# The last three groups of a graph network kernel: sums streamed 32 columns wide, and their place among the last updates

## The chip, the cores and the metric

The kernel runs on one core of one Trainium2 chip. The core has TensorE (PE in the profile, its weight loads shown apart as PEld), VectorE (DVE), ScalarE (ACT), GpSimd (POOL) and SyncE (SP, which here only issues transfers). Every engine works through its own list of instructions in order and waits on semaphores for the others. The metric is the device time of one execution in microseconds (us), as the median of several runs; less is better.

## The reference

One layer of message passing over 12,500 nodes with 64 features and 200,000 edges, which are sorted by destination, then a residual and a layer norm:

```python
msg_in     = concat([x[src], x[dst], edge_attr_32])            # 64 + 64 + 32 features
messages   = relu(msg_in @ mW1 + mb1) @ mW2 + mb2              # 160 -> 128 -> 64
aggregated = segment_sum(messages, dst, 12500)                 # 12500 x 64
update     = relu(concat([x, aggregated]) @ uW1 + ub1) @ uW2 + ub2
out        = layernorm(x + update)                             # over 64 features
```

All of it is float32. Because the sum over edges and the second matrix of the message network commute, the kernel sums the 128 hidden values of the edges per node and applies `mW2` afterwards, once per node.

## The kernel before, in words

**Groups.** The edges are cut into 1563 tiles of 128, and six tiles make a group: groups 0 to 260, the last with three tiles. Since destinations are sorted, the destinations of one tile lie within a window of 32 consecutive nodes. The rows of the sources are gathered from a table in DRAM on GpSimd's queue.

**A group's life.** `edge_part(s)` (L413, L416) makes the parts of the hidden values that come from the destination and the edge features, as products into PSUM (`pc`). `node_part(s)` adds the gathered source part; for the groups from 255 on VectorE does the addition itself (`added_here`, L452) and clips at zero (L455; for the short group 260 ScalarE clips, L457). `collect(s)` then sums the group's edges into their nodes: for each tile a product of a row of ones with the 0/1 selection matrix gives the counts (L502, tile `cnt`), and a product of the hidden values `h` (128 edges x 128 values, the loaded weights) with the selection (the streamed columns) gives the sums (L506, tile `sums`). In float32 each product appears as two records in the profile, so a full group's sums are x12. Where in `sums` the window lies is read from a list at run time.

**The streamed columns.** The 32 columns of a tile's selection lie in `band`. `widened` builds an access pattern that reads them and, `WIDE` - 1 = 2 further times, 32 columns of zeros from elsewhere in `band`, so that 96 columns are streamed and the 64 columns behind the window get zeros added.

**Updates.** The nodes are finished in 36 updates (K = 36; update u in the code). Update K-3 covers the nodes of groups 251 to 254, K-2 those of 255 to 257, K-1 (the last, 256 nodes wide) those of 258 to 260. An update goes through a chain of functions: `close_counts` and `close_sums` copy counts and sums from PSUM (L527, L533, VectorE); `carry(u+1)` hands what overlaps to the next update's sums (L521, L522, TensorE); `from_nodes` and `update` make the first layer from the nodes and counts (L565) and from the sums (L558); `activated` is the ReLU (L570, ScalarE, into `hTu`); `residual` makes the second layer and the residual (L578 from the nodes, L580 from `hTu`), centred, into the PSUM tile `cps`, which all updates share; `squares` (L587, ScalarE), `statistics` (L596, VectorE), `deviation` (L602, ScalarE) and `norm` (L608 and L610, VectorE) are the layer norm; `store` (L617) issues the store on SP's queue.

**What sets the order.** Nothing schedules these instructions: the order in which the functions are called is the order of each engine's list. Up to group 257 a loop makes it; for the last three groups (258 is `FINAL`) and the last three updates it is written out call by call. So a place in this list is a place in the queue of each engine that the called function uses.

Of the kernel before, what the change touches and what calls it, by code (L numbers as in the profile page):

```python
# [10 lines left out]
F32 = mybir.dt.float32  # L11
# [19 lines left out]
WIN = 32  # L31
# [17 lines left out]
WIDE = 3  # L49
# [9 lines left out]
def opener(t):  # L59

    return t - t % SUP % shared(t // SUP)
# [15 lines left out]
SBASE = (33556480, 33554432)  # L77
CBASE = 33566720
PACE = ((3, 0.474), (50, 0.501), (130, 0.479), (170, 0.465), (261, 0))
FINAL = 258  # L80
# [49 lines left out]
def gnn_kernel(ctx: ExitStack, tc: tile.TileContext, x1T, x, eT, e_rows, src, src_row, dst, dst_row, wlist, wrow, wnext, whalf,  # L130
# [24 lines left out]
    nc = tc.nc  # L155
# [8 lines left out]
    K = len(UPD)  # L164
# [53 lines left out]
    def tiles(s):  # L218
        return range(s * SUB, min((s + 1) * SUB, NT))
# [28 lines left out]
    with tc.tile_pool(name="work", bufs=2) as work, tc.manual_schedule():  # L248
# [172 lines left out]
        def node_part(s):  # L421

            n = len(tiles(s))
            added = None
            pc = pcs.pop(s)
            h = work.tile([P, 2, SUB // 2, DH], F32, name="h")
            if s < XG:
                xt = xs.pop(s)
                for i in range(n):
                    k, b = divmod(i, 2)  # L430
                    q = 64 * b
                    nc.tensor.matmul(pc[:, b, k, :], xt[q:q + 64, k, :], w1a[q:q + 64], start=False,
                                     stop=i + 2 >= n)
                nc.scalar.activation(h, pc, AF.Relu)
            else:
                a = xg.pop(s)[0].rearrange("p (b k) f -> p b k f", b=2)
                if s >= SUMMED:
                    added_here(s, n, h, a, pc)
                elif n == SUB:
                    m = SUB // 2 - (s in COPIED)  # L440
                    for b in range(2):
                        added = nc.tensor.matmul(pc[:, b, :m], ident, a[:, b, :m], start=False, stop=True)  # L442
                    late.append((h, pc))
            hs[s] = h
            return added

        def added_here(s, n, h, a, pc):

            m = SUB // 2 - (s in COPIED)
            blocks = [(slice(0, 2), m)] if n == SUB else parts(n)  # L450
            for b, m in blocks:
                nc.vector.tensor_tensor(h[:, b, :m], a[:, b, :m], pc[:, b, :m], op=ALU.add)  # L452
            for b, m in blocks:
                if n == SUB:
                    nc.vector.tensor_scalar(h[:, b, :m], h[:, b, :m], 0.0, None, op0=ALU.max)  # L455
                else:
                    nc.scalar.activation(h[:, b, :m], h[:, b, :m], AF.Relu)  # L457
            if n == SUB and m < SUB // 2:
                nc.vector.tensor_scalar(h[:, :, m:], pc[:, :, m:], 0.0, None, op0=ALU.max)
# [24 lines left out]
        def collect(s):  # L484

            n = len(tiles(s))
            g, j = divmod(s, SUP // SUB)
            k0 = j * SUB
            u = period[s]
            ends = s == NSUB - 1 or period[s + 1] != u  # L490
            if s == 0 or period[s - 1] != u:
                opened(u)
            ps, pn = sums[u]
            h = hs.pop(s)
            at = [t for t in listed(s) if t < NT]
            cs, ws = ([found[at.index(opener(t))] for t in tiles(s)]
                      for found in (places(wcnt, s, at, CBASE), places(woff, s, at, SBASE[u % 2])))
            pn8, ps8 = pn.bitcast(U8), ps.bitcast(U8)
            if s == 0 or period[s - 1] != u:
                nc.tensor.matmul(pn, zero_b[:, 0:1], zero_b, start=True, stop=False)  # L500
            for i in range(n):
                nc.tensor.matmul(pn8[:, bass.ds(cs[i] - CBASE, 4 * WIN)].bitcast(F32), one, SB[g][:, k0 + i, :, 1], start=False,  # L502
                                 stop=ends and i == n - 1)
            made = []
            for i in range(n):
                made.append(nc.tensor.matmul(ps8[:, bass.ds(ws[i] - SBASE[u % 2], 4 * WIDE * WIN)].bitcast(F32), h[:, i % 2, i // 2, :], widened(g, k0 + i),  # L506
                                        start=False, stop=ends and i == n - 1))
            return made

        def widened(g, t):  # L510

            a = g % 3 * SEL + t * WIN
            v = band[:, a:a + WIN]
            return bass.AP(v.tensor, v.offset, [v.ap[0], [(ZTOP - a) // 2, WIDE], [1, WIN]])

        def carry(u):
# [12 lines left out]
        def close_sums(u):  # L529

            ps, _ = sums.pop(u)
            n = UV if u + 1 < K else width(u)
            nc.vector.tensor_copy(sums_s[u % 2][:, :n], ps[:, :n])  # L533
            shut[u] = ps
# [25 lines left out]
        def from_nodes(u, pu=None):  # L560

            n = width(u)
            if pu is None:
                pu = psum.tile([DH, UW], F32, name="sums")[:, :n]
            nc.tensor.matmul(pu, uz, xw[u % 2][:, :n], start=True, stop=False)  # L565
            pus[u] = pu

        def activated(u):

            nc.scalar.activation(hT[:, :width(u)], pus.pop(u), AF.Relu, bias=ub1_s)  # L570
# [3 lines left out]
        def residual(u):  # L574

            py = cps[:, YC:].rearrange("p (i d) -> p i d", d=D)
            for i in range(blocks(u)):
                nc.tensor.matmul(py[:, i], xw[u % 2][:, i * P:(i + 1) * P], ux, start=i == 0, stop=False)  # L578
            for i in range(blocks(u)):
                nc.tensor.matmul(py[:, i], hT[:, i * P:(i + 1) * P], u2c, start=False, stop=i + 1 == blocks(u))  # L580
            ys[u] = py
# [23 lines left out]
        def norm(u):  # L605
            n, y, sd = blocks(u), ys.pop(u), sds.pop(u)
            rs = work.tile([P, UB], F32, name="rs")
            nc.vector.reciprocal(rs[:, :n], sd[:, :n])  # L608
            o = work.tile([P, UB, D], F32, name="y")
            nc.vector.tensor_tensor(o[:, :n], y[:, :n], rs[:, :n].unsqueeze(2).broadcast_to([P, n, D]), op=ALU.mult)  # L610
            us[u] = (us[u], o)
# [3 lines left out]
        def store(u):  # L615
            n0, o = us.pop(u)
            nc.sync.dma_start(out[bass.ds(n0, blocks(u) * P), :].rearrange("(c p) d -> p c d", p=P), o[:, :blocks(u)])  # L617
# [157 lines left out]
        for k, c in enumerate(range(0, NB, NCH)):  # L775
# [20 lines left out]
            if k in (5, 7):  # L796
                g = (k - 5) // 2
# [98 lines left out]
        for s in range(FINAL):  # L896
            g, j = divmod(s, SUP // SUB)
# [85 lines left out]
        deviation(K - 3)  # L983
        update(K - 2)
        activated(K - 2)
        node_part(FINAL + 1)
        norm(K - 3)
        store(K - 3)
        collect(FINAL)
        carry(K - 1)  # L990
        edge_part(FINAL + 2)
        node_part(FINAL + 2)
        residual(K - 2)
        squares(K - 2)
        statistics(K - 2)
        deviation(K - 2)
        collect(FINAL + 1)
        norm(K - 2)
        store(K - 2)
        collect(FINAL + 2)  # L1000
        close_counts(K - 1)
        close_sums(K - 1)
        from_nodes(K - 1)
        update(K - 1)
        activated(K - 1)
# [10 lines left out]
    with tc.If(flag > 0), tc.tile_pool(name="gen", bufs=1) as up:  # L1016
# [28 lines left out]
        with tc.For_i(0, NT, 1) as t:  # L1045
# [31 lines left out]
            h = up.tile([P, DH], F32, name="hg")  # L1077
# [104 lines left out]
```

## Time and profile before

| | |
|---|---|
| median of 3 runs | 2132.84 us (2132.43 to 2137.72) |
| the profiled execution | 2134.32 us in all, 2132.5 us from first to last instruction |
| TensorE busy | 1665.4 us, 78% of the span |
| ScalarE busy | 1583.4 us, 74% |
| GpSimd busy, VectorE busy | 1250.4 us, 59%, and 1162.9 us, 55% |
| mean granted TensorE clock | 0.786 |
| last 15 of these us | the stretch that the change touches |

The rows of the view in time read: start in us from the span's beginning, length in us, engine, line, operation, what is written from what, shapes, number of records; in brackets how long the engine was idle before and what ended that. In the chain of waits each row is one piece of the chain that ended last. A PEld row is a run of weight loads; the distance from its start to the start of the next row divided by its records is what one record of that group takes up on TensorE.

### The profile page before, as it was taken

The numbers are of one execution on the slowest core, as the hardware profiler recorded it, in microseconds if no ns is written. First come the engines' busy times: TensorE is split into PE (matmuls) and PEld (weight loads), VectorE is DVE, ScalarE is ACT, GpSimd is POOL, SyncE is SP. The second block draws the span as 40 slices with busy tenths as digits, with TensorE's granted clock in tenths as the row PEclk, the third lists the DMA queues.
The fourth block names the chain that finished last, engine by engine and source line by source line (L and its number), as shares of the span: only waits on it lengthen the run. The fifth ranks groups of instructions, "written<-read, shape, count | busy, mean of one in ns | idle before, by whom it ended". The sixth has DMA issues, their size and how long they took to land.

```text
span 2132.5 us, 48222 instructions
## 1 busy us (share of the span) xinstructions
PE 1665.4 (78%) x10730; PEld 1259.0 (59%) x10730; DVE 1162.9 (55%) x8400; ACT 1583.4 (74%) x8069; POOL 1250.4 (59%) x1330
## 2 busy tenths in 40 slices
PE   3676887787787787878777878878776888888888
PEld 2564665565565556656656656656555666656666
DVE  2436555555555565565555545555554556555555
ACT  4396977759769688788786877777876868787774
POOL 6665665666665665655655555565556566666660
PEclk8677787787786777777877778787887878788779
DMA  8623333322223232232222323333332333333332
GB/s 227 185 73 85 87 95 90 106 75 80 74 75 81 73 83 75 74 86 78 77 82 81 85 77 89 83 91 84 81 90 75 87 85 94 87 93 88 90 88 54
DMA packets 207647, 190.04 MB, mean 89 GB/s; under 512 B 57813, under 2 KB 173997, under 8 KB 207357
## 3 DMA queue, kind: packets, MB, share of 16 engines
q0 software_dynamic: 42272, 85.08, 15.6%
q1 hardware_dynamic: 150396, 92.86, 15.5%
q10 hardware_dynamic: 14690, 8.99, 1.5%
q8 instruction: 90, 1.47, 0.3%
q14 instruction: 199, 1.63, 0.3%
HBM read 168.76 MB, written 18.02 MB: 88 GB/s over the span
## 4 chain that ended last, share of the span: by engine, by line
PE 50%; issue 16%; DVE 12%; another core or an unknown queue 3%; DVEq 2%; POOL 0%; ACT 0%; DMA 0%; ACTq 0%; POOLq 0%
PE sums L506 16%; PE pc L442 12%; PE pc L413 10%; DVE xc L391 6%; DVE h L466 3%; PE cnt L502 2%; PE cps L580 2%; PE cps L578 2%; DVE l L275 2%; PE sums L565 2%; DVEq L359 2%; PE sums L558 1%; PE pc L416 1%; PE cnt L500 1%
## 5 line engine op out<-in xcount | busy, mean ns | idle before, releaser
L241 POOL DMA_INDIRECT xg<-tab_a,src_s x1273 | 1201.4, 944 | 809.4 <-issue 266.0
L383 ACT ACTIVATE xc<-xtop,xbot 128x1 f32 x7912 | 1501.3, 280 | 172.7 <-issue 149.4
L391 DVE TENSOR_TENSOR xc<-xtop,xbot 128x1 int32 x7576 | 634.7, 154 | 504.9 <-issue 489.6
L506 PE MATMUL sums<-band,h 128*128 128x96 f32 x3126 | 529.7, 322 | 143.1 <-issue 91.3
L506 PEld LDWEIGHTS sums<-band,h 128*128 128x128 f32 x3126 | 466.4, 228 | 172.9 <-issue 106.3
L442 PE MATMUL pc<-xg,band 128*128 128x256 f32 (+1 forms) x988 | 445.8, 581 | 29.1 <-issue 27.5
L413 PE MATMUL pc<-rhs,l 64*128 64x128 f32 x3126 | 366.8, 351 | 79.3 <-issue 66.1
L413 PEld LDWEIGHTS pc<-rhs,l 64*128 64x128 f32 x3126 | 290.0, 235 | 127.0 <-issue 94.9
L466 DVE TENSOR_SCALAR h<-pc 128x768 f32<-128x768 f32 x247 | 235.0, 952 | 167.8 <-remote 62.4
L442 PEld LDWEIGHTS pc<-xg,band 128*128 128x128 f32 x988 | 215.5, 241 | 145.1 <-issue 100.2
L502 PEld LDWEIGHTS <-one 128*1 128x1 bf16 x1563 | 59.0, 81 | 247.2 <-issue 242.7
L275 DVE TENSOR_TENSOR l<-l,cps 128x768 f32<-128x768 int32 (+1 forms) x134 | 127.0, 947 | 136.2 <-remote 31.8
L502 PE MATMUL cnt<-band,one 128*1 128x32 bf16 x1563 | 95.4, 180 | 69.9 <-issue 68.8
L587 ACT ACTIVATE y<-cps 128x256 f32<-128x256 f32 (+1 forms) x36 | 13.6, 379 | 162.2 <-issue 106.8
L570 ACT ACTIVATE hTu<-sums,ub_s 128x416 f32<-128x416 f32 (+1 forms) x36 | 21.6, 600 | 136.0 <-remote 41.7
L416 PE MATMUL pc<-band,xc 64*128 64x128 f32 x484 | 78.3, 314 | 14.5 <-issue 13.3
L283 DVE TENSOR_TENSOR band<-cps,drc 128x384 f32<-128x384 f32 x131 | 71.4, 545 | 20.1 <-PE pc L413 15.8
L675 PE MATMUL pb<-band,xtop 64*128 64x128 f32 x200 | 44.1, 383 | 48.4 <-issue 20.9
L416 PEld LDWEIGHTS pc<-band,xc 64*128 64x128 f32 x484 | 65.2, 228 | 15.6 <-issue 15.5
L675 PEld LDWEIGHTS pb<-band,xtop 64*128 64x128 f32 x200 | 37.4, 276 | 52.5 <-issue 28.7
L241 POOL DMA_INDIRECT xg<-in_x,src_s x48 | 48.0, 1000 | 25.6 <-issue 14.4
L580 PE MATMUL cps<-u2c,hTu 128*128 128x64 f32 x284 | 51.3, 329 | 10.1 <-issue 9.8
(108 smaller groups left out, 636.4 us busy)
## 6 DMA issues: line engine op xcount, KB each, us to landing
l<-in_dst_row SPq DMA_DIRECT2D x262, 96.0 KB
l<-in_eT SPq DMA_DIRECT2D x262, 96.0 KB
xg<-tab_a,src_s POOLq DMA_INDIRECT x1273
rhs<-tab_b SPq DMA_DIRECT2D x361, 32.0 KB
tab_b<-tb SPq DMA_DIRECT2D x13, 512.0 KB
rhs<-tab_b SPq DMA_DIRECT2D x387, 16.0 KB
tab_a<-tb ACTq DMA_DIRECT2D x12, 512.0 KB
out<-y SPq DMA_DIRECT2D x35, 128.0 KB
```

What stands on the lines that cost most here:

```text
L241: ins = nc.gpsimd.indirect_dma_start(out=a[:, i, :] if s < XG else a[:, i // 2, i % 2, :], out_offset=None, in_=A[:, :] if s >= XG else x[ ...
L275: nc.vector.tensor_tensor(l[r], l[r].bitcast(I32), node[r].unsqueeze(2).broadcast_to([r.stop - r.start, SUP // 2, P]), op=ALU.is_equal)
L383: nc.scalar.activation(o[:, e:e + 1], top.bitcast(F32), AF.Identity, bias=bot.bitcast(F32))
L391: nc.vector.tensor_tensor(o[:, e:e + 1].bitcast(I32), top.bitcast(I32), bot.bitcast(I32), op=ALU.bitwise_or)
L413: done = nc.tensor.matmul(pc[:, b, k, :], L[g][q:q + 64, m, :], rhs[g % 2][q:q + 64, w, :], start=k == 0, stop=ends and not copied)
L416: done = nc.tensor.matmul(pc[:, b, k, :], xc[s][q:q + 64], w1a[q:q + 64], start=False, stop=ends)
L442: added = nc.tensor.matmul(pc[:, b, :m], ident, a[:, b, :m], start=False, stop=True)
L466: nc.vector.tensor_scalar(h, pc, 0.0, None, op0=ALU.max)
L502: nc.tensor.matmul(pn8[:, bass.ds(cs[i] - CBASE, 4 * WIN)].bitcast(F32), one, SB[g][:, k0 + i, :, 1], start=False, stop=ends and i == n - 1)
L506: made.append(nc.tensor.matmul(ps8[:, bass.ds(ws[i] - SBASE[u % 2], 4 * WIDE * WIN)].bitcast(F32), h[:, i % 2, i // 2, :], widened(g, k0 + i),
L580: nc.tensor.matmul(py[:, i], hT[:, i * P:(i + 1) * P], u2c, start=False, stop=i + 1 == blocks(u))
L675: nc.tensor.matmul(pb[:, h, i, :], (xbot if h else xtop)[64 * h:64 * h + 64, (c + HB * h + i) * P:(c + HB * h + i + 1) * P], w[64 * h:64 * ...
```

## The change

Three edits, all in the stretch after the loop. `widened` takes the width as an argument, and in the groups from `FINAL` on (258, 259 and 260) it returns the 32 columns of the selection alone. `norm(K-3)` is called before `node_part(FINAL+1)` instead of after it. `collect(FINAL+1)` is called before `residual(K-2)` instead of after `deviation(K-2)`, and `norm(K-2)` and `store(K-2)` are called after `close_sums(K-1)` instead of before `collect(FINAL+2)`. The change computes the same values: what falls away are additions of zeros.

```diff
@@ collect
             for i in range(n):
-                made.append(nc.tensor.matmul(ps8[:, bass.ds(ws[i] - SBASE[u % 2], 4 * WIDE * WIN)].bitcast(F32), h[:, i % 2, i // 2, :], widened(g, k0 + i),
+                wide = 1 if s >= FINAL else WIDE
+                made.append(nc.tensor.matmul(ps8[:, bass.ds(ws[i] - SBASE[u % 2], 4 * wide * WIN)].bitcast(F32), h[:, i % 2, i // 2, :], widened(g, k0 + i, wide),
                                         start=False, stop=ends and i == n - 1))
             return made
 
-        def widened(g, t):
+        def widened(g, t, wide):
 
             a = g % 3 * SEL + t * WIN
             v = band[:, a:a + WIN]
+            if wide == 1:
+                return v
             return bass.AP(v.tensor, v.offset, [v.ap[0], [(ZTOP - a) // 2, WIDE], [1, WIN]])
@@ the calls after the loop
         update(K - 2)
         activated(K - 2)
+        norm(K - 3)
         node_part(FINAL + 1)
-        norm(K - 3)
         store(K - 3)
         collect(FINAL)
         carry(K - 1)
         edge_part(FINAL + 2)
         node_part(FINAL + 2)
+        collect(FINAL + 1)
         residual(K - 2)
         squares(K - 2)
         statistics(K - 2)
         deviation(K - 2)
-        collect(FINAL + 1)
-        norm(K - 2)
-        store(K - 2)
         collect(FINAL + 2)
         close_counts(K - 1)
         close_sums(K - 1)
+        norm(K - 2)
+        store(K - 2)
         from_nodes(K - 1)
         update(K - 1)
         activated(K - 1)
```

Lines below the first edit move by one to three in the changed kernel: L506 becomes L507, and L527, L533, L558, L565, L570, L578, L580, L587, L596, L602, L608, L610 and L617 become L530, L536, L561, L568, L573, L581, L583, L590, L599, L605, L611, L613 and L620.

On TensorE, behind the carry into update K-1 and the edge part of group 260 (L413), the list before has the residual of K-2 (L578, L580; `xw_75` is K-2's node tile):

```order
L521 MATMUL sums<-sums_s_73,band 128x32
L522 ISA
L522 MATMUL cnt<-xw_75,band 1x32
L413 MATMUL pc<-rhs_78,l_81 128x128 x3
L578 MATMUL cps<-ux,xw_75 128x64 x4
L580 MATMUL cps<-u2c,hTu 128x64 x4
L502 LDWEIGHTS one
```

And now, with the counts (L502) and sums (L507) of group 259 done, the residual (L581, L583) comes between them and the counts of group 260:

```order
L502 MATMUL cnt<-band,one 1x32
L507 MATMUL sums<-band,h 128x32 x6
L581 MATMUL cps<-ux,xw_75 128x64 x4
L583 MATMUL cps<-u2c,hTu 128x64 x4
L502 LDWEIGHTS one
```

The residual of K-2 has moved behind group 259's six tiles, and those write 32 columns where they wrote 96.

On VectorE, from the add and clip of group 259 (L452, L455) to the two copies of the last update (L527, L533) the list before is:

```order
L452 TENSOR_TENSOR h<-xg,pc 128x768
L455 TENSOR_SCALAR h<-h 128x768
L608 RECIPROCAL rs<-sd 128x4
L610 TENSOR_TENSOR y<-cps,rs 128x256
L452 TENSOR_TENSOR h<-xg,pc 128x256
L452 TENSOR_TENSOR h<-xg,pc 128x128
L596 TENSOR_REDUCE ss<-y 128x4
L608 RECIPROCAL rs<-sd 128x4
L610 TENSOR_TENSOR y<-cps,rs 128x256
L527 COPY xw_76<-cnt 1x256
L533 COPY sums_s_74<-sums 128x256
```

And now:

```order
L611 RECIPROCAL rs<-sd 128x4
L613 TENSOR_TENSOR y<-cps,rs 128x256
L452 TENSOR_TENSOR h<-xg,pc 128x768
L455 TENSOR_SCALAR h<-h 128x768
L452 TENSOR_TENSOR h<-xg,pc 128x256
L452 TENSOR_TENSOR h<-xg,pc 128x128
L599 TENSOR_REDUCE ss<-y 128x4
L530 COPY xw_76<-cnt 1x256
L536 COPY sums_s_74<-sums 128x256
L611 RECIPROCAL rs<-sd 128x4
L613 TENSOR_TENSOR y<-cps,rs 128x256
```

K-3's norm (the first reciprocal and product) now stands ahead of group 259's add, and K-2's norm behind the last update's copies; K-2's reduction (L596, now L599) is still ahead of the copies. The lists of ScalarE and SP have the same rows in the same order.

## The prediction

> **What bounds the kernel now.** I read the page first, then the chain of waits, then the order in time of one engine after another over the last 20 us, since the change touches nothing before them.
>
> ```profile
> span 2132.5 us, 48222 instructions
> PE 1665.4 (78%) x10730; PEld 1259.0 (59%) x10730; DVE 1162.9 (55%) x8400; ACT 1583.4 (74%) x8069; POOL 1250.4 (59%) x1330
> ```
>
> Over the whole span TensorE is the busiest engine, but what the change is worth must be read from its own stage. The chain of waits over the last 15 us, as start, length and work:
>
> ```profile
> 2119.66 1.03 PE cps L578 x8
> 2120.70 0.89 PE cps L580 x8
> 2121.59 0.23 PE cnt L502 x6
> 2121.83 1.51 PE sums L506 x12
> 2123.33 0.16 PE cnt L502 x3
> 2123.49 0.85 PE sums L506 x6
> 2124.34 0.02 issue
> 2124.37 0.43 DVE sums_s L533
> ...
> 2124.85 0.71 PE sums L558 x2
> ...
> 2125.64 0.48 ACT hTu L570
> ...
> 2128.13 0.29 DVE y L610
> ```
>
> Up to 2124.34 TensorE works without a gap: residual of update K-2 (L578, L580), then the sums of groups 259 (x12: six tiles, two records each) and 260 (x6: three tiles). From there on it is a relay of single steps with one engine working at a time: VectorE's copy of the sums, the last update's products, ScalarE, products, squares, deviation, norm and store. So two things can set the end: how early TensorE gets through its list, and how early VectorE is free for the two copies L527 and L533. Whatever delays the copies or L558 is paid in full.
>
> **The change part by part: narrower streams.** 15 products (30 records) stream 32 columns instead of 96. What one record costs is its distance to the next weight load (PEld rows; at the full clock):
>
> ```profile
> 2110.39 0.30 PEld L502 LDWEIGHTS <-one 128*1 128x1 bf16 x6
> 2110.73 1.41 PEld L506 LDWEIGHTS sums<-band,h 128*128 128x128 f32 x12
> 2112.07 0.97 PEld L578 LDWEIGHTS cps<-ux,xw 128*128 128x128 f32 x8
> ...
> 2118.95 0.52 PEld L413 LDWEIGHTS pc<-rhs,l 64*128 64x128 f32 x6
> 2119.59 0.97 PEld L578 LDWEIGHTS cps<-ux,xw 128*128 128x128 f32 x8
> 2120.48 0.97 PEld L580 LDWEIGHTS cps<-u2c,hTu 128*128 128x128 f32 x8
> 2121.52 0.19 PEld L502 LDWEIGHTS <-one 128*1 128x1 bf16 x6
> 2121.75 1.41 PEld L506 LDWEIGHTS sums<-band,h 128*128 128x128 f32 x12
> 2123.26 0.11 PEld L502 LDWEIGHTS <-one 128*1 128x1 bf16 x3
> 2123.42 0.74 PEld L506 LDWEIGHTS sums<-band,h 128*128 128x128 f32 x6
> ```
>
> Twelve records of L506 with 96 columns take (2112.07 - 2110.73) / 12 = 0.112 us each; eight of L578 with 64 columns take (2120.48 - 2119.59) / 8 = 0.111. A third fewer columns buy nothing: the weight load of 128x128, the same in both, sets the pace. 32 columns therefore save nothing between records, only part of the tail of a group's last one, where somebody waits for its end. The bounds: at least nothing; at most as if cost went with columns, 30 x 0.112 x 2/3 = 2.2 us. I take the end at nothing, because the row with 64 columns lies between 96 and 32 and shows no slope, plus at most 0.08 us of tail for group 260 (64 of 96 columns of a 0.11 us record).
> [...]
>
> **The order on TensorE.** Group 259's products now stand before the residual of K-2, not behind it. Group 259 starts where the residual stood, 2119.59. Its counts (L502) precede the sums by 2110.73 - 2110.39 = 0.34, so its sums start at 2119.93. Followed by L578 a group takes 1.34 (2110.73 to 2112.07): residual at 2121.27, that is 1.68 later than before. The residual and its switch to L502 take 2121.52 - 2119.59 = 1.93: counts of 260 at 2123.20. 0.16 to the sums (2123.26 to 2123.42): 2123.36, 0.06 sooner than now. With the shorter tail, the last product ends 0.06 to 0.14 sooner. That is all TensorE gains: the same records stand there.
>
> **The order on VectorE and ScalarE.** The relay around update K-2 in time, then the last update's first steps:
>
> ```profile
> 2115.03 0.30 ACT L602 ACTIVATE sd<-ss,eps 128x4 f32<-128x4 f32 x1 [0.49 <-DVE ss L596]
> 2121.69 0.38 ACT L587 ACTIVATE y<-cps 128x256 f32<-128x256 f32 x1 [0.92 <-PE cps L580]
> 2122.11 0.42 DVE L596 TENSOR_REDUCE ss<-y 128x4 f32<-128x256 f32 x1 [1.79 <-ACT y L587]
> 2122.89 0.18 DVE L608 RECIPROCAL rs<-sd 128x4 f32<-128x4 f32 x1 [0.36 <-ACT sd L602]
> 2123.16 0.42 DVE L610 TENSOR_TENSOR y<-cps,rs 128x256 f32<-128x256 f32 x1
> 2123.53 0.41 DVE L527 COPY xw<-cnt 1x256 f32<-1x256 f32 x1
> 2124.37 0.42 DVE L533 COPY sums_s<-sums 128x256 f32<-128x256 f32 x1 [0.43 <-PE sums L506]
> ...
> 2124.16 0.62 PE L565 MATMUL sums<-xw,band 128*128 128x256 f32 x2
> 2124.85 0.70 PE L558 MATMUL sums<-sums_s,w2u 128*128 128x256 f32 x2
> 2125.38 0.55 PE L578 MATMUL cps<-ux,xw 128*128 128x64 f32 x4
> 2126.17 0.66 PE L580 MATMUL cps<-u2c,hTu 128*128 128x64 f32 x4 [0.23 <-ACT hTu L570]
> ```
>
> Here is the price. The squares of K-2 wait for the residual's end and move by its 1.68: from 2121.69 to 2123.37. The reduction L596 goes from 2122.11 to 2123.79, and in VectorE's queue it still stands ahead of both copies. The counts it blocks are done about when L527 ran before, 2123.5. An operation of this size holds VectorE 0.37 (L610 to L527), so L527 starts at 2124.16 instead of 2123.53 and L533 at about 2124.52 instead of 2124.37 (+0.15). L565 needs the counts (0.41 of copy and some 0.05 to be seen): 2124.62; L558 stands behind L565's two records, which take 0.62 to their end, of which L558's stream may overlap up to half: 2124.93 to 2125.24. The copied sums let L558 start at 2124.52 + 0.48 = 2125.00 at the soonest, against 2124.85 now. I take 2125.05. Term: **+0.2 us**, between +0.1 (the tail of a shortened group reaches the squares too, and the reduction with them) and +0.4 (all of L565's 0.62).
>
> Norm and store of K-2, now behind both copies, start at 2124.52 + 0.36 = 2124.88 (K-2's deviation is ready at 2124.24 + 0.30) and end near 2125.6. The last update's L578 writes the very `cps` columns that this norm reads, so it waits: 2125.6 instead of 2125.38, ends at 2126.2. L580 needs hTu, at 2126.17 + 0.2 = 2126.37. Cost nothing, with 0.2 to spare; without that cover, up to what the norm is late.
>
> Norm of K-3 moves ahead of group 259's add on VectorE. Its deviation ends at 2115.03 + 0.30 = 2115.33; reciprocal and product (0.27 + 0.42) hold VectorE until 2116.0, so the add and the clip of group 259 end about 1 us later, near 2117.6. Group 259's products now need them at 2119.93: covered by 2.3 us. Its store leaves a microsecond sooner and nobody waits for it.
>
> The stores: three are issued from SP, and each one's wait list holds the landing of the one before, as their rows overlap. The first row is the issue of the last two; the second is the DMA traffic in 40 slices of 0.075 us from 2123.5.
>
> ```profile
> 2123.61 5.21 SPq L617 DMA_DIRECT2D out<-y  x2
> ...
> GB/s 0 0 0 0 0 0 0 0 0 0 0 0 218 0 96 205 232 215 218 222 215 171 65 0 0 10 7 7 10 10 10 10 7 20 17 0 0 0 0 0
> ```
>
> K-2's store is issued at 2123.61 and its last bytes move in the last slice above zero, the 35th, at 2126.1: 2.5 us. Issued at 2125.6, it lands at 2128.1. The last store is ready after L610, 2128.13 + 0.29 + 0.2 = 2128.6. Covered by 0.5, and the wait costs nothing.
>
> **Sum:** span 2132.5 + 0.2 = 2132.7; the profiled execution took 2134.32 in all, the median of the runs shown is 2132.84 (2132.43 to 2137.72). Forecast 2133.0 us, which means no change: 0.3%, 6.4 us, is about the least that can be told from the scatter here.
>
> **The rivals.**
> 1. *Columns set the pace.* Then group 258's products and 259's, both now ahead of the squares, shed 0.9 each (12 x 0.112 x 2/3); the relay starts 1.8 sooner less the 0.2: 2131.2. For it: the products are shortened to a third. Against: 0.112 beside 0.111 with 64 columns. Chance 0.08.
> 2. *The clock, the one that ends slower.* In these rows of the view by stretches the granted clock is the third figure from the end. The tail runs at the full clock; other stretches ran at half, with L506's twelve loads in 2.64, 0.22 apart, instead of 0.11.
>
> ```profile
> 2097.00:2100.70 3.70, 0.09 (x1) 0.08 (x1) 2.80 (x7) 1.68 (x9) 0.00 (x0) 1.00 0.15 42
> 2102.10:2105.40 3.30, 3.30 (x10) 2.23 (x10) 1.07 (x3) 0.00 (x0) 0.00 (x0) 0.50 0.16 42
> 2117.10:2126.20 9.10, 8.81 (x78) 7.71 (x74) 2.43 (x8) 1.91 (x6) 0.00 (x0) 1.00 0.12 31
> ...
> 2071.27 2.64 PEld L506 LDWEIGHTS sums<-band,h 128*128 128x128 f32 x12
> ```
>
> Narrow streams leave the array idle for more of each record. If the grant falls for one stretch of 3.3 us, half of its work is late: +1.6, 2134.6; if it falls at 2118 and stays, the 6.3 us up to 2124.3 double: 2139.3. It decides only if the grant falls before 2124. For it: a half-clock stretch follows right behind TensorE's 3.7 us gap at 2097 to 2100.7. Against: residuals with 64 columns ran within full-clock stretches. Chance 0.08.
> [...]
> 3. *A store waits.* If K-2's store needs 4 us instead of 2.5, it lands at 2129.6, and the last store waits 1.0: 2134.0. Against: the same store took 2.5 here. Chance 0.06.
> 4. *The change does less than its words.* "Sooner" holds for K-3's norm alone, which nobody waits for; K-2's goes later. If the reduction finds VectorE early enough after all, TensorE's 0.1 is the whole effect: 2132.7. Chance 0.18.
>
> **How the numbers follow.** The forecast has 0.60, and the four rivals 0.40 between them. All cases but the long half-clock stretch stay within 2131 to 2135; runs of one and the same kernel scatter from 2132.43 to 2137.72, so the range is 2131.0 to 2137.8: rival 1 below, the scatter above. Faster by over 0.3% would need 6 us, more than any case gives: 0.02, for scatter. Slower by over 0.3%: rival 2 at its end or scatter, 0.03. Same: 0.95.
>
> **What would show it.** In the changed kernel's trace, the 32-column records should stand 0.111 apart (0.08 or less proves rival 1); L580 of K-2 ends near 2123.3 relative to an unchanged 2117.1; the reduction runs right up to the copy of the counts, which is then about 0.6 later; L558 starts 0.1 to 0.4 later; L578 of the last update waits for the norm without delaying L580; the clock in the last 9 us stays 1.00. The prediction is wrong if L558 starts sooner, if the last store waits, or if the time leaves the range.

## The result, and the profile after

| | before | after |
|---|---|---|
| median of 13 runs | 2132.84 us (2126.55 to 2137.72) | 2138.5 us (2131.05 to 2142.91) |
| the profiled execution | 2134.32 us | 2131.05 us |
| its span | 2132.5 us | 2129.3 us |
| last opening of counts (L500) to the end of the span | 15.78 us | 18.70 us |

The change made the kernel slower, by a ratio of 1.0027 with a 95% interval of 1.0016 to 1.0038. That lies within 0.3% of no change, but it is clear of the scatter, and the median lies outside the forecast's range.

The profiled execution of after is its shortest, and shorter than that of before. Ahead of the last 20 us both programs are the same, and yet one execution differs from another there: in the nine traces with this list on chips of this speed the last L500 starts between 2110.4 and 2123.0. So spans can't be compared here. What can be compared is the stretch from one fixed instruction to the end. I take L500, which opens the counts of the last update; it is in every kernel, and nothing ahead of it on TensorE differs. This stretch is called **the tail** below.

The first lines of the page of after. Of the 18 us that TensorE is busier (1683.7, before 1665.4) only 3.2 lie in the tail (13.1 against 9.9); the null kernel of the experiments, whose instructions are those of before, shows 1677.5.

```profile
span 2129.3 us, 48222 instructions
PE 1683.7 (79%) x10730; PEld 1277.0 (60%) x10730; DVE 1162.6 (55%) x8400; ACT 1582.1 (74%) x8069; POOL 1252.5 (59%) x1330
```

The view by stretches shows where the tail differs. Columns: stretch and its length in us; busy time and records of TensorE, its weight loads, VectorE, ScalarE, GpSimd; then the granted clock, the share of the DMA engines, GB/s. First before, from its L500 at 2116.68:

```profile
2116.68:2121.68 5.00, 5.00 (x52) 4.53 (x51) 1.04 (x3) 1.18 (x3) 0.00 (x0) 1.00 0.10 26
2121.68:2126.68 5.00, 4.71 (x39) 3.93 (x35) 1.80 (x5) 1.15 (x3) 0.00 (x0) 1.00 0.12 30
```

The same two stretches of after, from its L500 at 2110.59, and the remainder:

```profile
2110.59:2115.59 5.00, 4.84 (x51) 4.36 (x50) 1.41 (x4) 1.17 (x3) 0.00 (x0) 1.00 0.11 27
2115.59:2120.59 5.00, 5.00 (x26) 4.77 (x26) 1.04 (x3) 0.68 (x2) 0.00 (x0) 0.51 0.01 3
2120.59:2129.28 8.69, 3.27 (x12) 2.65 (x10) 1.38 (x6) 1.05 (x3) 0.00 (x0) 0.50 0.10 25
```

In the first 5 us both do about 50 records. In the second before does 39 and still has idle time, while after does 26 in five full microseconds: the granted clock, the third figure from the end, has gone from 1.00 to 0.51. It stays at half to the end. In before it falls only at 2129.3, behind the last product.

The weight loads of after, in time:

```profile
2111.03 1.41 PEld L507 LDWEIGHTS sums<-band,h 128*128 128x128 f32 x12
2112.37 0.30 PEld L524 LDWEIGHTS sums<-sums_s,band 128*128 128x128 f32 x2
...
2113.97 1.41 PEld L507 LDWEIGHTS sums<-band,h 128*128 128x128 f32 x12
2115.31 1.46 PEld L581 LDWEIGHTS cps<-ux,xw 128*128 128x128 f32 x8
2116.64 1.83 PEld L583 LDWEIGHTS cps<-u2c,hTu 128*128 128x128 f32 x8
2118.59 0.11 PEld L502 LDWEIGHTS <-one 128*1 128x1 bf16 x3
2118.76 1.36 PEld L507 LDWEIGHTS sums<-band,h 128*128 128x128 f32 x6
2119.99 0.55 PEld L568 LDWEIGHTS sums<-xw,band 128*128 128x128 f32 x2
```

With 32 columns twelve records take (2112.37 - 2111.03) / 12 = 0.112 us each, as with 96. The first two narrow groups pass at this pace (2111.03 and 2113.97). The residual behind them (L581, L583) begins at it; L583's eight take (2118.59 - 2116.64) / 8 = 0.24 where before had 0.13 (2120.48 to 2121.52 of the rows in the prediction). Group 260's six take 0.205 each. From 2113.97 to the end of group 260 TensorE has no gap, and behind the fall a record costs nearly twice as much.

VectorE's two copies and the last update follow as late as that makes them:

```profile
2119.17 0.42 DVE L599 TENSOR_REDUCE ss<-y 128x4 f32<-128x256 f32 x1 [4.95 <-ACT y L590]
2119.51 0.40 DVE L530 COPY xw<-cnt 1x256 f32<-1x256 f32 x1
2120.29 0.42 DVE L536 COPY sums_s<-sums 128x256 f32<-128x256 f32 x1 [0.38 <-PE sums L507]
...
2125.17 0.29 DVE L613 TENSOR_TENSOR y<-cps,rs 128x128 f32<-128x128 f32 x1
```

The copy of the sums waits again for TensorE (0.38 <-PE sums), not for VectorE's queue. The last norm ends 2125.17 + 0.29 - 2110.59 = 14.87 behind L500; before it was 2128.13 + 0.29 - 2116.68 = 11.74.

### The profile page after: what moved, and what is told of

It is laid out like the page before. It is cut to its first block, busy times and chain, and to the rows that moved or that the text cites. A ratio compares the mean times of both kernels' runs of the same rounds, so it can differ in the third digit from the quotient of the medians.

```text
span 2129.3 us, 48222 instructions
## 1 busy us (share of the span) xinstructions
PE 1683.7 (79%) x10730; PEld 1277.0 (60%) x10730; DVE 1162.6 (55%) x8400; ACT 1582.1 (74%) x8069; POOL 1252.5 (59%) x1330
## 5 line engine op out<-in xcount | busy, mean ns | idle before, releaser
L507 PE MATMUL sums<-band,h 128*128 128x96 f32 x3126 | 533.1, 325 | 140.4 <-issue 97.0
L507 PEld LDWEIGHTS sums<-band,h 128*128 128x128 f32 x3126 | 473.6, 232 | 170.0 <-issue 113.8
L442 PE MATMUL pc<-xg,band 128*128 128x256 f32 (+1 forms) x988 | 455.2, 591 | 29.4 <-issue 26.9
L413 PE MATMUL pc<-rhs,l 64*128 64x128 f32 x3126 | 373.0, 358 | 70.0 <-issue 58.9
L413 PEld LDWEIGHTS pc<-rhs,l 64*128 64x128 f32 x3126 | 294.4, 240 | 117.3 <-issue 87.6
L442 PEld LDWEIGHTS pc<-xg,band 128*128 128x128 f32 x988 | 221.3, 247 | 147.4 <-issue 99.8
L502 PEld LDWEIGHTS <-one 128*1 128x1 bf16 x1563 | 58.3, 81 | 229.6 <-issue 224.1
L502 PE MATMUL cnt<-band,one 128*1 128x32 bf16 x1563 | 94.7, 180 | 64.7 <-issue 64.0
L590 ACT ACTIVATE y<-cps 128x256 f32<-128x256 f32 (+1 forms) x36 | 13.7, 380 | 170.4 <-issue 109.3
L573 ACT ACTIVATE hTu<-sums,ub_s 128x416 f32<-128x416 f32 (+1 forms) x36 | 21.6, 601 | 138.4 <-remote 64.9
L416 PE MATMUL pc<-band,xc 64*128 64x128 f32 x484 | 83.0, 330 | 17.3 <-issue 15.6
L583 PE MATMUL cps<-u2c,hTu 128*128 128x64 f32 x284 | 52.2, 337 | 6.3 <-issue 6.1
```

The lines of the kernel that those rows point to most:

```text
L413: done = nc.tensor.matmul(pc[:, b, k, :], L[g][q:q + 64, m, :], rhs[g % 2][q:q + 64, w, :], start=k == 0, stop=ends and not copied)
L416: done = nc.tensor.matmul(pc[:, b, k, :], xc[s][q:q + 64], w1a[q:q + 64], start=False, stop=ends)
```

## The experiments

The theories, by the letters that the expectations use. **C**: the narrow streams bring the granted clock down, and the tail runs at half. **O**: the moved calls cost the time. **N**: neither does; the difference is that of how a program was loaded or placed, which any rebuilt kernel would show. A digit behind a letter marks a later form, which the text there spells out.

The experiments were measured in four sets, each on one chip and each with the kernel before beside it. "Difference" below is that of the mean times against this kernel before, with a standard error. Two of the four sets ran on chips where the kernel before takes about 1686 us, not 2133, with a higher granted clock (0.87 to 0.90 over the runs of the kernel before, against 0.77 to 0.80) and less idle time of TensorE that is put down to issue (ahead of the products of the sums 0.3 us in a run of the change there, 118.9 in the null run); times are compared only within a set.

**Null: three blank lines.** The kernel before, rebuilt.

> The kernel before with three blank lines put in: the same program. If the 5.7 us between the two kernels came from the change (theory C, the clock, and theory O, the order), this run is within 2 us of the kernel before. If equal programs differ by some 5 us from one loading to the next (theory N), it may stand 3 us or more off, either way. It sets how much the other three can tell.

Measured: 2136.31 us beside 2135.51, ratio 1.0005 (0.9991 to 1.0019), difference +0.1 ± 1.1. Tail 15.81, clock full to the last product. N has nothing for it here.

**The narrow streams alone.** The order stays that of before.

```diff
-                made.append(... 4 * WIDE * WIN ... widened(g, k0 + i) ...
+                wide = 1 if s >= FINAL else WIDE
+                made.append(... 4 * wide * WIN ... widened(g, k0 + i, wide) ...
```

> Only the narrow streams: groups 258 to 260 stream 32 columns, all calls stay in the order before. Theory C (the granted clock falls behind the narrow streams, as in the one profile of the changed kernel, where it went to half at 2115.7 us, 4.7 us after they began, and stayed there to the end): +3 to +6 us, and its profile shows half clock from some point behind group 258 to the end. Theory O (the order costs): 0 to -0.3 us and the full clock up to L580. Theory N: like the null run.

Measured: 2135.78 us, ratio 1.0004 (0.9993 to 1.0016), difference +1.2 ± 0.95: not told apart by time. By trace it is: tail 19.25 us. By stretches, from L500 at 2121.24:

```profile
2121.24:2126.24 5.00, 5.00 (x44) 4.59 (x43) 1.04 (x3) 1.17 (x3) 0.00 (x0) 0.88 0.10 26
2126.24:2131.24 5.00, 5.00 (x31) 4.69 (x30) 1.44 (x4) 0.68 (x2) 0.00 (x0) 0.50 0.12 29
```

Half the clock from 3.85 us behind L500, at 2125.09, with the order untouched. At that time group 259's products have not begun:

```profile
2125.00:2125.20 0.20, 0.20 (x4) 0.20 (x4) 0.00 (x0) 0.20 (x2) 0.00 (x0) 0.71 0.00 0
```

```profile
2127.19 2.77 PE L507 MATMUL sums<-band,h 128*128 128x32 f32 x12
```

**The order alone.** Only the calls after the loop are moved; all streams are 96 wide.

```diff
+        norm(K - 3)
         node_part(FINAL + 1)
-        norm(K - 3)
...
+        collect(FINAL + 1)
         residual(K - 2)
...
-        collect(FINAL + 1)
-        norm(K - 2)
-        store(K - 2)
         collect(FINAL + 2)
         close_counts(K - 1)
         close_sums(K - 1)
+        norm(K - 2)
+        store(K - 2)
```

> Only the moved calls: the streams keep 96 columns. Theory C: +0.1 to +0.4 us, what the prediction worked out for the reduction ahead of the two copies, and the full clock to the last products. Theory O: most of the 5.7 us. Theory N: like the null run.

Measured: 2136.98 us, ratio 1.0002 (0.9988 to 1.0016), difference +0.7 ± 1.0; tail 15.79. Its stretches from L500 at 2117.49, then VectorE, then TensorE in time:

```profile
2117.49:2122.49 5.00, 4.82 (x50) 4.35 (x50) 1.42 (x4) 1.18 (x3) 0.00 (x0) 1.00 0.10 26
2122.49:2127.49 5.00, 4.47 (x35) 3.85 (x34) 1.58 (x5) 1.15 (x3) 0.00 (x0) 1.00 0.04 9
```

```profile
2124.74 0.42 DVE L596 TENSOR_REDUCE ss<-y 128x4 f32<-128x256 f32 x1 [3.61 <-ACT y L587]
2125.08 0.40 DVE L527 COPY xw<-cnt 1x256 f32<-1x256 f32 x1
2125.41 0.40 DVE L533 COPY sums_s<-sums 128x256 f32<-128x256 f32 x1
```

```profile
2120.65 0.31 PE L502 MATMUL cnt<-band,one 128*1 128x32 bf16 x6 [0.18 <-issue]
...
2124.32 0.91 PE L506 MATMUL sums<-band,h 128*128 128x96 f32 x6
...
2125.54 0.70 PE L565 MATMUL sums<-xw,band 128*128 128x256 f32 x2 [0.31 <-DVE xw L527]
...
2126.07 0.59 PE L558 MATMUL sums<-sums_s,w2u 128*128 128x256 f32 x2
```

The clock stays full. The relay is the one the prediction described: the reduction, then both copies without a gap, and L565 waits for the counts. L558 starts 2126.07 - 2117.49 = 8.58 behind L500, before 8.17: +0.41. So O has its mechanism, but no time that can be measured.

**The whole change, beside these.**

> The change as it is, once more beside the other three on one chip. Theories C and O: +3 to +7 us again; C also half clock behind the narrow streams in this second profile. Theory N: no better separated from the kernel before than the null run is.

Measured: 2140.15 us, ratio 1.0019 (1.0004 to 1.0034), difference +4.7 ± 1.0. Tail 17.67, half the clock from 6.35 us behind L500.

**The change with 64 columns in the last groups**, in the moved order.

```diff
-                wide = 1 if s >= FINAL else WIDE
+                wide = 2 if s >= FINAL else WIDE
...
-            return bass.AP(v.tensor, v.offset, [v.ap[0], [(ZTOP - a) // 2, WIDE], [1, WIN]])
+            return bass.AP(v.tensor, v.offset, [v.ap[0], [(ZTOP - a) // 2, wide], [1, WIN]])
```

> The changed order with 64 columns (one repetition of zeros) in groups 258 to 260, between the 32 of the change and the 96 before. Theory C (the clock follows the columns streamed, by the two runs with the full clock at 96 and the three with half clock at 32): either the full clock to the last products and a stretch of 16.1 us from the last opening of the sums (L473) to the end, as in the order-only run, or half clock late in it and 16.1 to 18; time between +0 and +3 us. If the 32 columns cost by something else than the clock, the stretch is about 17 us at the full clock.

Measured: 2132.37 us beside 2132.17, ratio 1.0001 (0.9987 to 1.0014), difference -0.1 ± 1.4. Tail 15.90:

```profile
2118.80:2123.80 5.00, 4.84 (x51) 4.36 (x50) 1.41 (x4) 1.17 (x3) 0.00 (x0) 1.00 0.10 27
2123.80:2128.80 5.00, 4.44 (x35) 3.85 (x34) 1.58 (x5) 1.15 (x3) 0.00 (x0) 1.00 0.04 10
```

One step back in width, with order and number of records as in the change, and the clock is full again. It isn't the edited access pattern as such that costs.

**32 columns in every group**, order before.

```diff
-                made.append(... 4 * WIDE * WIN ... widened(g, k0 + i) ...
+                wide = 1
+                made.append(... 4 * wide * WIN ... widened(g, k0 + i, wide) ...
```

> 32 columns in all 261 groups, calls in the order before; the zeros are not streamed anywhere. Theory C: the mean granted clock falls well below 0.78 (to 0.5 to 0.7), and the kernel is slower by more than 2%, over 40 us. If the narrow streams only matter at the end of the program, or cost by something else, the mean clock stays within 0.77 to 0.80 and the time within 10 us.

Measured: 2148.03 us, ratio 1.0069 (1.0048 to 1.009), difference +15.3 ± 2.6. The same 1400 us of the middle, first of before, then of this kernel:

```profile
200.00:1600.00 1400.00, 1116.83 (x6999) 835.23 (x7000) 780.87 (x5865) 1088.35 (x5683) 839.36 (x890) 0.78 0.31 83
```

```profile
200.00:1600.00 1400.00, 1216.51 (x6992) 920.53 (x6991) 780.14 (x5854) 1085.26 (x5674) 839.38 (x888) 0.67 0.30 83
```

The same number of records takes 100 us more of TensorE, since the mean clock is 0.67, not 0.78. Yet the whole execution is only 15 us longer, where theory C had expected over 40. So most of what TensorE loses in the loop isn't paid for in time; I take it that it falls into TensorE's waits for other engines, which no run here tests.

**The narrow streams alone, and the change, again.**

> The narrow streams alone, a second time, to set the term's size: its first profile had a stretch from L473 to the end of 19.6 us against 16.1, its timed runs only +1.2 us. Theory C: stretch 18 to 20 us again, half clock from 3.4 to 7 us behind the start of group 258's products, time +2 to +4 us. Theory O2 (narrow streams and order only cost together): time 0 to +1 us.

> The change a third time, beside the narrow streams alone. Theory C: stretch 18 to 20 us, half clock from 3.4 to 7 us behind the start of group 258's products, time +2 to +4 us, and no more than 1.5 us away from the narrow run. Theory O2: +4 to +6 us, 3 us or more above the narrow run, though its stretch from L473 is no longer.

Measured: narrow 2132.83 us, 1.0011 (0.9997 to 1.0024), +1.85 ± 1.3, tail 16.62, half clock from 7.78; the change 2135.54, 1.0013 (1.0002 to 1.0025), +3.3 ± 1.2, tail 18.83, half clock from 5.05. The two lie 1.4 us apart, with an error of about as much, which tells C (up to 1.5) from O2 (3 or more) poorly. Over the runs so far the fall comes at another place of the tail each time, between 3.85 and 7.78 us behind L500.

**Other widths in every group**, on a chip of the faster kind. For 128 columns there must be room behind the sums, so the updates are 384 nodes wide (`UN`), and a control has that alone. With 128 the zeros in the middle are streamed twice.

```diff
# 64 columns
-WIDE = 3
+WIDE = 2
# control
-UN = 416
+UN = 384
# 128 columns
-UN = 416
+UN = 384
-WIDE = 3
+WIDE = 4
-            return bass.AP(v.tensor, v.offset, [v.ap[0], [(ZTOP - a) // 2, WIDE], [1, WIN]])
+            return bass.AP(v.tensor, v.offset, [v.ap[0], [(ZTOP - a) // 2, 2], [(ZTOP - a) // 2, 2], [1, WIN]])
```

> 64 columns in all 261 groups (one repetition of zeros instead of two), order before. With 32 columns in all groups the mean granted clock was 0.694 and the time +0.7%, with 96 columns 0.78 to 0.79. Theory C (the clock follows the columns streamed, in steps): a mean clock between 0.70 and 0.78 and +0.1 to +0.5%. If only a stream as short as 32 columns matters: 0.78 and within 0.1%.

> The kernel before with updates of at most 384 nodes instead of 416, which makes 39 updates instead of 36, 96 columns: only the comparison for the next run. Three more updates of some 4 to 5 us on TensorE each: 0 to +13 us, mean clock 0.78 to 0.79.

> 128 columns in all groups (the zeros in the middle streamed twice), with updates of 384 nodes, since a window and three strips of zeros behind it have to end within the 512 columns of the sums. Theory C: a mean clock above that of the run with 384 nodes and 96 columns by 0.01 to 0.06, and 2 to 10 us faster than it; whether it beats the kernel before depends on what the three updates cost. If the clock does not follow the columns beyond 96, the same clock and the same time as with 384 nodes and 96 columns.

> The change a fourth time, for the size: the timed differences so far are 5.8, 4.7 and 3.3 us, those of the narrow streams alone 1.2 and 1.9, the stretch from L473 to the end 18.0 to 19.1 us and 16.9 to 19.6. Theory C alone (the end of the program sets the whole difference): +2 to +4 us. Theory O2 (something more than the end): +4 to +6 us again with a stretch below 19.2 us.

Measured, beside 1685.25 us: 64 columns 1697.43, ratio 1.0054 (1.0032 to 1.0076); control 1686.67, 1.001 (0.9996 to 1.0025); 128 columns 1686.55, 1.0006 (0.9993 to 1.0018); the change 1688.8, 1.0021 (1.0009 to 1.0032), +3.5 ± 0.8, tail 18.38, half clock from 4.86. The middle, in this order 64 columns, control, 128:

```profile
200.00:1600.00 1400.00, 1213.12 (x8991) 941.52 (x9020) 983.03 (x7422) 1344.90 (x7149) 1055.83 (x1118) 0.85 0.38 106
```

```profile
200.00:1600.00 1400.00, 1178.53 (x9148) 925.18 (x9182) 988.48 (x7480) 1361.41 (x7238) 1058.57 (x1120) 0.90 0.38 107
```

```profile
200.00:1600.00 1400.00, 1163.16 (x9158) 917.85 (x9192) 992.82 (x7512) 1365.70 (x7263) 1057.85 (x1120) 0.91 0.38 107
```

The clock rises with the columns: 0.85, 0.90, 0.91. From 64 to 96 that buys time; from 96 to 128 it doesn't. (The clocks that the texts above expect are those of the slower kind of chip. The 2 to 10 us that C expected of 128 columns did not come.) The change's fourth run, +3.5 us, lies within the +2 to +4 of C alone.

**The change with work added.** Behind groups 258 and 259 TensorE also adds two products of zeros, 512 columns in bf16.

```diff
+            for _ in range(2 * (FINAL <= s < NSUB - 1)):
+                nc.tensor.matmul(ps, zero_b[:, :P], zero_b, start=False, stop=False)
             return made
```

> The change with 32 columns, plus two products of zeros with 512 columns behind the sums of group 258 and two behind those of 259, 0.2 us each: more work on TensorE, the same sums. Theory C (activity): the full clock to the last products, a stretch from L500 to the end of 16.3 to 17.0 us against 18.4 of the change and 15.8 of the kernel before, and 1 to 3 us faster than the change run beside it. If the 32 columns themselves bring the clock down: half clock as in the change, a stretch of 18.5 to 20 us, slower than the change by up to 1.5 us.

Measured: 1684.86 us beside 1686.44, ratio 0.999 (0.9975 to 1.0004), difference -1.55 ± 0.8; the change, measured beside it (below), is at +3.1 ± 1.05. That is 4.7 apart, more than the 1 to 3 expected. Tail 16.31. The stretches, of which the second starts 5 us behind L500, then the added products behind group 258:

```profile
1667.30:1672.30 5.00, 5.00 (x51) 4.35 (x51) 1.36 (x4) 1.17 (x3) 0.94 (x1) 1.00 0.21 53
1672.30:1677.30 5.00, 4.64 (x36) 3.99 (x33) 1.58 (x5) 0.97 (x3) 0.00 (x0) 1.00 0.01 3
```

```profile
1669.11 0.59 PE L510 MATMUL sums<-band 128*128 128x512 bf16 x2
```

This is the run that decides between "32 columns are slow by themselves" and "32 columns bring the clock down". The narrow products and the order are those of the change, TensorE does more, not less, and the clock stays at 1.00. The cost of the change is gone. Against before it isn't faster: the interval reaches 1.0004.

**The change with only group 258 narrow.**

```diff
-                wide = 1 if s >= FINAL else WIDE
+                wide = 1 if s == FINAL else WIDE
```

> Changed order, 32 columns in group 258 alone, 96 in 259 and 260. If one narrow group in a window of 3.4 us is enough: half clock, a stretch of 17 to 19 us. If it takes two, one behind the other: the full clock to the last products, a stretch of 15.8 us, and a time within 1.5 us of the kernel before.

> The change a fifth time, beside the filled one and the narrow streams alone: +3 to +5 us, a stretch from L500 of 17.5 to 19 us, half clock from 4.8 to 6.5 us behind it.

> The narrow streams alone a third time. If they cost less than the change because the clock falls later in some executions: half clock from anywhere between 3.8 and 8 us behind L500, a stretch between 16.5 and 19.3, +1 to +2.5 us. If the two differ by chance alone: +3 to +5 us like the change.

Measured: one narrow group 1687.67, ratio 1.0007 (0.9991 to 1.0023), +0.2 ± 1.2, tail 15.91; the change 1690.5, 1.0014 (1.0002 to 1.0026), +3.1 ± 1.05, tail 18.96; the narrow streams alone 1687.11, 0.9999 (0.9984 to 1.0014), +0.7 ± 1.0, tail 17.15. First one narrow group, then the change, each from its L500:

```profile
1663.30:1668.30 5.00, 5.00 (x53) 4.55 (x52) 1.51 (x2) 0.56 (x1) 2.42 (x3) 1.00 0.35 89
1668.30:1673.30 5.00, 4.46 (x35) 3.85 (x34) 2.20 (x7) 1.77 (x5) 0.00 (x0) 1.00 0.08 20
```

```profile
1674.91:1679.91 5.00, 5.00 (x50) 4.55 (x49) 0.62 (x2) 1.18 (x3) 0.00 (x0) 0.93 0.17 40
1679.91:1684.91 5.00, 5.00 (x26) 4.82 (x26) 0.75 (x3) 0.68 (x2) 0.00 (x0) 0.50 0.01 3
```

The time of the narrow streams alone lies below the +1 to +2.5 expected, its tail within the range. In this execution the clock stayed at 1.00 behind one narrow group of 1.4 us. In the first run of the narrow streams it fell at 2125.09, when one narrow group had passed; group 259's products began at 2127.19. The 3.41 us ahead of that fall hold group 258, the carry, an edge part and half of the 64-column residual (2121.68 to 2125.09). What tells the two cases apart may be where the changes of the clock happen to lie (see the next section), and isn't tested. (The 3.4 us that the expectation calls a window are the length of the half-clock stretch from 2102.0 to 2105.4 in the trace of before; that what is streamed in one such stretch decides is an assumption.)

**All tails together**, one profiled execution each, in us behind L500:

| | half clock from | L558 (in the change L561) starts | last norm ends | end of span |
|---|---|---|---|---|
| before | 12.6, behind the products | 8.17 | 11.74 | 15.78 |
| null | not in the products | 8.16 | 11.74 | 15.81 |
| order alone | not in the products | 8.58 | 12.06 | 15.79 |
| 64 columns | not in the products | 8.57 | 12.05 | 15.90 |
| only 258 narrow | not in the products | 8.33 | 11.80 | 15.91 |
| change, filled with zeros | not in the products | 9.02 | 12.50 | 16.31 |
| the change, five executions | 5.1, 6.35, 5.05, 4.86, 4.31 | 9.36 to 10.76 | 13.76 to 15.16 | 18.70, 17.67, 18.83, 18.38, 18.96 |
| narrow alone, three | 3.85, 7.78, 6.5 | 8.06 to 11.13 | 12.61 to 15.52 | 19.25, 16.62, 17.15 |

All eight tails in which groups 258 and 259 both stream 32 columns, with no zeros added, have the half clock in their products; no other tail of the table has.

## Why the prediction was wrong, point by point

**The step that failed: the clock.** The prediction wrote "the clock in the last 9 us stays 1.00" and gave 0.08 to its rival 2, "Narrow streams leave the array idle for more of each record." The fall of the clock in that rival is what happened; that the array's idle time is its cause was an assumption, which no run shows. Its price for a fall that stays, "the 6.3 us up to 2124.3 double: 2139.3", assumed a fall 1.3 us behind L500. The falls came at 4.3 to 6.35, so less work doubled; on the other hand that price left out the last update's products, which run at half as well (from L558's start to the end of the last norm 4.40 us, before 3.57). The mean tail of the five executions of the change is 18.5, which is +2.7. In the first comparison the tail's +2.9 alone would have left the time at 2135.8, inside the range; what took the median out of it is a remainder that the trace doesn't place ("What stays open", below). The fall had been named, and its row, the half clock behind the 3.7 us gap, had been quoted. The misjudgement was the argument against it, "residuals with 64 columns ran within full-clock stretches": those residuals stand between 96-column groups, and the row said nothing about a stretch in which the sums are narrow too. In the sum the clock stood at nothing.

Where exactly the fall comes isn't set by the program alone: over the five executions of the change it lies 4.31 to 6.35 us behind L500. Read in steps of 0.1 us, the clock in the trace of before changes between 2060 and 2132 at 2067.9, 2078.1, 2102.0, 2105.4 and 2129.3: distances of 3, 7, 1 and 7 times 3.41 us. In the trace of after it changes between 2050 and 2129 at 2057.7, 2064.5, 2081.6, 2085.0 and 2115.7: 2, 5, 1 and 9 times 3.41. So in these two traces the changes lie on a grid, and L500 stands at another place of it in each, with the last fall 12.6 us behind it in before and 5.1 in after. If the 3.41 holds in the other executions too, which is an estimate from these two, the fall behind the products with only group 258 narrow, at about 12.96 (a mean clock of 0.75 over the last 5.91 us), puts a point at about 2.7 behind L500, so that group shared its stretch with 416 and 512 columns wide products ahead of it; in the first run of the narrow streams, with the fall at 3.85, the stretch began at 0.44, with the narrow group itself (2121.68).

In that run the clock fell within a stretch of 5.00 us that TensorE was busy throughout, so no gap between products stood in the 3.85 us ahead of the fall. The runs fit a measure that counts how much is streamed, not whether records follow one another: with four products of zeros added to the change the clock stayed at 1.00. How much it takes they leave open.

**Narrower streams save nothing between records: right.** 0.112 with 32 columns as with 96; rival 1 is refuted by that spacing. What didn't follow is that they therefore cost nothing.

**The order on VectorE and TensorE: mechanism right, size at the upper bound.** The term was "+0.2 us" with bounds +0.1 and +0.4; alone it measured +0.41 at L558, and +0.32 at the end of the norm (12.06 against 11.74). Two sizes made it so. The copy of the counts (L527) starts 7.59 behind L500 where 7.48 was forecast (2124.16 - 2116.68), as TensorE's list ends 0.08 later than before and not 0.06 sooner: the gap of 0.18 in the rows of the order alone, which the trace puts down to issue. And L558 stands 0.53 behind L565's start (2126.07 - 2125.54), where 0.43 was reckoned (2125.05 - 2124.62). In the whole tail it vanishes all the same (15.79 against 15.78), because the last store, behind the norm, took 3.73 and not 4.04. Why it did isn't known, and the timed difference of +0.7 ± 1.0 can tell neither.

**Norm of K-2 behind the copies: right.** In time, the order alone:

```profile
2125.93 0.43 DVE L610 TENSOR_TENSOR y<-cps,rs 128x256 f32<-128x256 f32 x1
...
2126.51 0.57 PE L578 MATMUL cps<-ux,xw 128*128 128x64 f32 x4
2126.77 0.47 ACT L570 ACTIVATE hTu<-sums,ub_s 128x256 f32<-128x256 f32 x1 [1.27 <-PE sums L558]
...
2127.29 0.66 PE L580 MATMUL cps<-u2c,hTu 128*128 128x64 f32 x4 [0.22 <-ACT hTu L570]
```

The norm ends at 2126.36, L578 starts behind it and ends at 2127.08, and L580 waits for `hTu` all the same: 0.2 to spare, as forecast.

**Norm of K-3 sooner, and the stores: right, hidden.** In the change, group 259's clip and the last store:

```profile
2110.86 0.56 DVE L455 TENSOR_SCALAR h<-h 128x768 f32<-128x768 f32 x1
```

```profile
2125.49 0.37 SPq L620 DMA_DIRECT2D out<-y  x1
```

The clip ends at 2111.42 and its products begin at 2113.97. The last store is issued 0.03 behind the end of its norm, 2125.46: rival 3 is refuted. Of rival 4 the first half is right, K-2's norm comes later and not sooner; the second isn't, since the reduction did hold up the copies, as the order alone shows (2124.74 to 2125.08).

**What stays open.** Over the five comparisons the change costs +3.95 ± 0.46 us (5.8, 4.7, 3.3, 3.5, 3.1, weighted by their errors), narrow streams alone +1.15 ± 0.6 (1.2, 1.85, 0.7). The tails explain +2.7 and +1.9. About 1.2 us of the change's time, some 2.6 of its standard errors with the tails' own scatter left aside, has no place in the trace. By time the change and the narrow streams alone lie 2.8 apart, by tail 0.8, though order alone costs nothing that can be measured (+0.7 ± 1.0): whether the two together cost more than the clock explains (O2) isn't settled. One profiled execution for each run, with a scatter of several us ahead of the tail, can't show where the remainder sits, and whether it is real is open too.

## What to carry to other kernels

Here, at the full clock, the records of the sums stood 0.112 us apart with 96 streamed columns and with 32, so narrower streams saved nothing between them; and in all eight tails where groups 258 and 259 streamed 32 columns, with no zeros added, the granted clock fell to 0.50 in the products, in the first run of the narrow streams within 5.00 us in which TensorE showed as fully busy. Before narrowing streams at a place where TensorE sets the end, look at the granted clock by stretches and at what stands beside that place, and ask what in it is still wide. The padding that looks like waste may be what holds the clock: here zeros streamed on purpose took the change's cost away again (-1.55 ± 0.8 us with them, +3.1 ± 1.05 without).

## What the hardware showed that I had not expected

- Full busy time and half the clock went together: 26 records in 5.00 busy us against 39 in 4.71 at the full clock, with much the same kinds of products.
- Products of zeros counted: with four of them (two take 0.43 us, from 1669.11 to L526's start at 1669.54) the clock stayed at 1.00.
- The clock also fell without narrow streams. In the tail of the 128-column kernel TensorE stood 2.02 us for a norm, and the clock was at half from 1670.2 on, 0.9 us after the wait had ended, with the widest streams of all; that the wait was the cause isn't tested.

```profile
1669.28 1.17 PE L578 MATMUL cps<-ux,xw 128*128 128x64 f32 x8 [2.02 <-DVE y L610]
```

```profile
1664.28:1670.20 5.92, 3.90 (x37) 3.43 (x38) 2.02 (x4) 0.53 (x1) 3.60 (x4) 1.00 0.21 58
1670.20:1677.00 6.80, 6.80 (x38) 6.33 (x38) 2.05 (x6) 1.30 (x4) 0.00 (x0) 0.50 0.15 39
```

- The same program took about 2133 us on two chips and 1686 on two others. In the groups of TensorE's work one difference is plain: for L506 (L507 in the change) the first figure behind `issue` below is idle time in which TensorE waited for nothing that the profile shows, 118.9 us on the one kind and 0.3 on the other. What causes it isn't known. First the null kernel, then the fourth run of the change, on a chip of the faster kind:

```profile
L506 PE MATMUL sums<-band,h 128*128 128x96 f32 x3126 | 543.8, 328 | 165.0 <-issue 118.9 <-DVE h L466 27.7 <-DVE xc L391 17.0
```

```profile
L507 PE MATMUL sums<-band,h 128*128 128x96 f32 x3126 | 463.3, 304 | 127.3 <-DVE h L466 126.8 <-issue 0.3
```
